# Narrow attention heads, software-pipelined: the next tile's first scores amid the products with V, the 1/sum and the projection one tile later, keys and queries in other PSUM banks

## The chip, the cores and the metric

The kernel runs on one core of a Trainium2 chip, as one program. The metric is the device time of one execution in microseconds (us). The engines are TensorE (PE; its weight loads are shown as PEld), VectorE (DVE), ScalarE (ACT), GpSimd (POOL) and SyncE (SP). SP computes nothing; it issues most of the DMAs. PSUM is the memory that matmuls write to, in banks; all the other on-chip data stands in SBUF.

## The reference, cut to what matters

Four layers run on x of shape (4, 512, 128) with a context of shape (4, 154, 128). Each layer is a cross attention and then a mixture of eight experts, both added to x. The change touches the attention of layer 1 alone:

```python
def _L1_xattn_ref(values, keys, queries, mask, Wv, Wk, Wq, Wo, bo):
    HEADS = 16                                   # E = 128, so D = 8
    v = values.reshape(N, -1, H, D)              # values = keys = context
    k = keys.reshape(N, -1, H, D)
    q = queries.reshape(N, Sq, H, D)             # queries = layernorm(x)
    v = jnp.einsum('nlhd,od->nlho', v, Wv)
    k = jnp.einsum('nlhd,od->nlho', k, Wk)
    q = jnp.einsum('nqhd,od->nqho', q, Wq)
    energy = jnp.einsum('nqhd,nkhd->nhqk', q, k)
    energy = jnp.where(mask == 0, jnp.float32(-1e+20), energy)
    attn = jax.nn.softmax(energy * (1.0 / E ** 0.5), axis=3)
    out = jnp.einsum('nhqk,nkhd->nqhd', attn, v).reshape(N, Sq, E)
    return out @ Wo.T + bo
```

The feed-forward part behind it sends every token to the best of eight experts (layer 1) or the best two (layers 0, 2, 3), with gate logits, a rank within the expert, and a weighted sum of what comes back.

## The kernel before, in words

**Tiles.** An attention works on tiles of 128 queries: four tiles (NI = 4) in each of four batches (B = 4), sixteen in all. Layer 1 has the narrow heads (8 dims each), layers 2 and 3 the wide ones (64 dims); they have a period function each, and share the class `Tile`. What a narrow tile goes through:

- `score(g)`, three groups: 6, 6 and 4 heads into one buffer `sc` of two PSUM banks. PE first writes the additive mask by a product with the identity (L1137) and then adds the queries times the keys (L1146). The keys `kz` stand eightfold, each copy masked to one head's dims of the eight in its half.
- `most(g)`: DVE takes the negated maximum over the 154 keys (L291, result `nm`).
- `exp(g)`: one ScalarE exponential for each head (L305), with the row's sum in `rs`.
- `short()`: ScalarE copies the last 26 keys of all heads together (L316). `inverse()`: DVE takes 1/sum (L327).
- `replicate()`: PE transposes 1/sum (L332), DVE copies it out of PSUM (`rT`, L334), SP sends it to DRAM eightfold (`rd`, L339) and back into SBUF (`rep`, L340), so that each of the 128 output rows has its head's 1/sum.
- `turn_ends()`, `turn(n)`, n = 0 to 3: PE transposes the probabilities, four 128x128 blocks into one bank `tr` (L355, L368). `take_ends`, `take(n)`: DVE copies the bank to SBUF (`tails`, `pT`; L261).
- `by_v_ends()`, `by_v(n)`: PE multiplies by the values into one bank `av` (L387, L405).
- `scaled()`: DVE multiplies by 1/sum (`aT`, L412). `project()`: PE multiplies by Wo (L422). `residual()`: DVE adds the bias and then x (L1160, L1161).

**PSUM.** Three pools share the banks: `ps_sc`, two buffers of two banks, `ps_tr` and `ps_av`, two buffers of one bank each. Who asks for a buffer waits until the one given out two calls earlier has been read.

**Order.** `attend_all` writes the order of PE, ACT and DVE by hand (`tc.manual_schedule`): each of these engines takes its instructions in program order, while SP's and POOL's are placed by a scheduler with a simulated time. `narrow_period(new, old, nxt, ...)` is one step of the loop over tiles: it does the rest of tile `new` (its groups 1 and 2; its group 0 was scored in the period before), the transposes and products of the tile before it, `old`, and the first scores of the tile after it, `nxt`. Four callbacks put other work into a period:

- `middle()` and `after()` each take one step of the work beside the attention (`beside.step`): the combine of the layer before for batches 2 and 3 (L953), the statistics of the layernorm (L224), the routing of the first half (gate logits L665, rank matmuls L692 and L694, choice and weights on DVE).
- `parts()` prepares the next batch, one part for each tile of the batch now running: `masks` (load L1091, conversion to an additive mask `madd` L1093), `xn` and `values` (L1111 to L1126), `xnT` (the transposed normalized x), and `keys_queries` (L1101 to L1109). This last one multiplies the context by Wk and x by Wq into the two banks of one `sc` buffer; DVE spreads the keys out under the head masks (`kz`, L1107) and ScalarE scales the queries (`qT`, L1109).
- `queries()` does nothing in this layer.

After the loop, outside the part with the order by hand, a last `narrow_period(None, last)` does the transposes, products and projection of the sixteenth tile, and the scheduler mixes it with the first steps of the experts.

Of the kernel before, what the change touches and what calls it, by code (L numbers as in the profile page):

```python
# [13 lines left out]
AF = mybir.ActivationFunctionType  # L14
ALU = mybir.AluOpType
# [6 lines left out]
S2 = 154  # L22
# [24 lines left out]
def tile_xattn_moe_stack(ctx: ExitStack, tc: tile.TileContext, a: dict, out: bass.AP):  # L47
# [10 lines left out]
    nc = tc.nc  # L58
# [37 lines left out]
    def bc(ap, axis, n):  # L96

        v = ap.unsqueeze(axis)
        shape = list(v.shape)
        shape[axis] = n  # L100
        return v.to_broadcast(shape)
# [42 lines left out]
    mask8 = const.tile([P, 8], F32, name="mask8")  # L144
# [42 lines left out]
    ctxT = const.tile([P, B, S2], F32, name="ctxT")  # L187
# [241 lines left out]
    def nothing():  # L429
        pass  # L430

    def narrow_period(new, old, nxt=None, middle=nothing, queries=nothing, parts=nothing, after=nothing):

        if new:  # L440
            new.score(1)
        if old:
            old.turn_ends()
            old.turn(0)
        if new:
            new.most(1)
            new.exp(0)
            new.exp(1)
        if old:
            old.take_ends("v")  # L450
            old.take(0, "v")
            old.by_v_ends()
            old.turn(1)
            old.take(1, "v")
        if new:
            new.score(2)
        if old:
            old.turn(2)
            old.by_v(0)
            old.by_v(1)  # L460
        if new:
            new.most(2)
            new.exp(2)
        if old:
            old.take(2, "v")
            old.turn(3)
            old.by_v(2)
            old.take(3, "v")
            old.by_v(3)
            old.scaled(0)  # L470
        middle()
        parts()
        if nxt:
            nxt.score(0)
            nxt.most(0)
        if new:
            new.short()
            new.inverse()
        queries()
        if new:  # L480
            new.replicate()
        if old:
            old.project()
            old.residual()
        after()

    def wide_period(new, old, nxt=None, middle=nothing, queries=nothing, parts=nothing, after=nothing):

        if new:
            new.score(0)  # L490
            new.score(1)
        if old:
            old.by_v_ends()
        if new:
            new.most(0)
            new.most(1)
            new.exp(0)
        if old:
            for n in (1, 2):
                old.turn(n)  # L500
                old.take(n, "v")
            old.by_v(0)
            old.by_v(1)
            old.turn(3)
            old.take(3, "v")
            old.by_v(2)
        if new:
            new.score(2)
            new.exp(1)
            new.most(2)  # L510
            new.exp(2)
# [12 lines left out]
        if old:  # L524
            old.project()
            old.residual()
        if new:
            new.turn_ends()
            new.take_ends("s")
            new.turn(0)  # L530
            new.take(0, "s")
        after()
# [526 lines left out]
    def layer1_setup():  # L1059
        dh = D // H  # L1060
        scale = 1.0 / D**0.5
        bd = {}
# [22 lines left out]
        def prepare(b, found):  # L1085
# [13 lines left out]
                at.xnT = transposed(at.xn)  # L1099

            def keys_queries():  # L1101
                sc = ps_sc()
                nc.tensor.matmul(sc[:, 0, 0:S2], bd["Wk"], ctxT[:, b, :], start=True, stop=True)
                nc.tensor.matmul(sc[:, 1, :], bd["Wq"], at.xnT, start=True, stop=True)

                at.kz = p2.tile([P, 8, S2], F32, tag="k", name="kz")
                nc.vector.tensor_tensor(at.kz, bc(sc[:, 0, 0:S2], 1, 8), bc(mask8, 2, S2), ALU.mult)  # L1107
                at.qT = p3.tile([P, S], F32, tag="t8", name="qT1")
                nc.scalar.activation(at.qT, sc[:, 1, :], AF.Copy, scale=scale)  # L1109

            def values():  # L1111
                vp = ps_av()
# [162 lines left out]
    def attend_all(layer, prepare, found, at, beside):  # L1275

        old = None
        period = narrow_period if layer == 1 else wide_period
        with tc.manual_schedule(engines=ordered):
            new = Tile(at, 0)
            if layer == 1:
                new.score(0)
                new.most(0)
            for b in range(B):
                new_at = prepare(b + 1, found) if b < B - 1 else None
                for i in range(NI):  # L1290
                    at_n, i_n = (at, i + 1) if i < NI - 1 else (new_at, 0)
                    nxt = Tile(at_n, i_n) if at_n else None
                    step = nothing if (b, i) in ((0, 0), (0, 1), (2, 0)) else beside.step

                    def queries(i=i, at=at):
                        if i < NI - 1:
                            at.queries(i + 1)

                    def parts(i=i, new_at=new_at):
                        if new_at:  # L1300
                            for part in new_at.parts[i]:
                                part()
                            if i == NI - 1:
                                new_at.queries(0)

                    def after(b=b, i=i, step=step):
                        step()
                        if b == 1 and i == 0:
                            beside.finish()
                            found.update({k: stats(x[k], layer == 2) for k in range(2, B)})  # L1310

                    period(new, old, nxt, step, queries, parts, after)
                    if b == 2 and i == 0:
                        beside = Steps(route(layer, 0, *gates[layer]))
                    old, new = new, nxt
                at = new_at
        return beside.finish(), old

    out_v = out.rearrange("b (i p) d -> b p i d", p=P)
    prepare = setups[0]()  # L1320
# [3 lines left out]
    for layer in range(4):  # L1324
        w2 = load_down(layer)
        if layer == 0:
            routed, last = [attend_first(layer, prepare, found)], None
        else:
            routed, last = attend_all(layer, prepare, found, at, beside)
            routed = [routed]  # L1330
        row_transfers()
        if layer < 3:
            prepare = setups[layer + 1]()
        first = Steps(experts(layer, 0, routed[0], w2)).step(2)
        if last:
            (narrow_period if layer == 1 else wide_period)(None, last)
        second = Steps(route(layer, 1, *gates[layer]))
        while not second.done:
            second.step(2)
# [55 lines left out]
```

## Time and profile before

| What | Value |
|---|---|
| Median of 5 runs | 1323.34 us (1318.14 to 1331.25) |
| Profiled execution | 1324.8 us, its span 1322.9 us |
| Mean granted PE clock | 0.93 |
| PE busy | 1096.5 us (83%) |
| PEld busy | 902.0 us (68%) |
| DVE busy | 748.4 us (57%) |
| ACT busy | 589.2 us (45%) |
| POOL busy | 252.8 us (19%) |
| HBM traffic over the span | 95 GB/s |

Busy shares are means over a span in which layers with different limits follow each other; the stretch of the layer that the change touches has to be cut out by time. The granted clock is a share of PE's full speed: at 0.50 a matmul takes twice as long. In a list by lines, `aT<-av,rep` says that `aT` was computed from `av` and `rep`. In a list of waits and in a timeline, an arrow with an engine and a name says whose result ended the idle time. Lines such as L261 (copies) and L291 (maxima) belong to helpers which all attention layers use, so their totals hold layers 2 and 3 too.

### The profile page before, as it was taken

To read this page: it belongs to the slowest core of one execution; us is meant where nothing else is said; L and a number is where in the kernel's file an instruction comes from. 1 tells how busy PE (TensorE), PEld (TensorE's weight loads), DVE (VectorE), ACT (ScalarE), POOL (GpSimd) and SP (SyncE) were. 2 spreads that over 40 slices of the span, in tenths; PEclk is the share of its full clock that TensorE was granted. 3 is DMA by queue.
4 is the path that set the end of the run, shared out by engine and by line. 5 is a ranking of instruction groups with operands and counts; after the bars stand their busy time and mean duration, and the time that the engine had idled before them with its cause. 6 is when DMAs were issued, how large, how long until landed. Compare 5 with 4: busy or idle time off the path is not lost.

```text
span 1322.9 us, 26947 instructions
## 1 busy us (share of the span) xinstructions
PE 1096.5 (83%) x9435; PEld 902.0 (68%) x9435; DVE 748.4 (57%) x2057; ACT 589.2 (45%) x2290; POOL 252.8 (19%) x281
## 2 busy tenths in 40 slices
PE   4875987887777778898999999867899999899881
PEld 2765877764334446787787787756778888789781
DVE  5663645557667566343676767424367576746442
ACT  1213443455454445446566556222466565533230
POOL 2032213104000020221000004045040000402424
PEclk8887999998898789999999999889899999999996
DMA  7023675551001122543121223445331111235762
GB/s 221 1 69 108 188 229 156 164 182 45 18 10 37 41 64 67 154 121 95 40 48 35 51 53 105 112 136 155 121 74 33 48 36 34 83 89 157 204 184 63
DMA packets 136995, 126.80 MB, mean 96 GB/s; under 512 B 13466, under 2 KB 116511, under 8 KB 136479
## 3 DMA queue, kind: packets, MB, share of 16 engines
q1 hardware_dynamic: 129695, 110.39, 30.1%
q0 software_dynamic: 7168, 14.69, 3.8%
q8 instruction: 77, 1.26, 0.4%
q14 instruction: 55, 0.45, 0.1%
HBM read 101.31 MB, written 23.72 MB: 95 GB/s over the span
## 4 chain that ended last, share of the span: by engine, by line
PE 37%; DVE 7%; DMA 7%; issue 3%; ACT 3%; POOL 2%; SPq 0%; POOLq 0%; DVEq 0%; ACTq 0%
PE sc L608 5%; PE tr L368 4%; PE tr L422 4%; PE av L405 4%; PE sc L875 4%; DMA w<-in_up 4%; PE av L902 3%; PE sc L593 3%; PE av L387 2%; ACT probs L305 2%; DVE nm L291 2%; POOL yg L935 2%; PE sc L557 1%; DMA yg<-ybuf,su 1%; DVE aT L412 1%
## 5 line engine op out<-in xcount | busy, mean ns | idle before, releaser
L305 ACT ACTIVATE probs<-sc,nm 128x154 f32<-128x154 f32 x768 | 287.0, 403 | 167.9 <-DVE nm L291 167.7
L875 PE MATMUL sc<-tokT,w 128*128 128x128 f32 x1528 | 213.0, 288 | 32.2 <-DMA w<-in_up 25.6
L875 PEld LDWEIGHTS sc<-tokT,w 128*128 128x128 f32 x1528 | 191.9, 200 | 46.6 <-DMA w<-in_up 13.7
L291 DVE TENSOR_REDUCE nm<-sc 128x6 f32<-128x924 f32 x144 | 143.2, 1010 | 85.2 <-PE sc L608 49.7
L902 PE MATMUL av<-w,hT 128*128 x1160 | 172.5, 283 | 11.1 <-DVE hT L891 9.2
L305 ACT ACTIVATION_READ_ACCUMULATOR probs<-sc,nm 128x1 f32 x768 | 168.2, 219 | 0.0
L902 PEld LDWEIGHTS av<-w,hT 128*128 128x128 f32 x1160 | 149.2, 194 | 21.5 <-DVE hT L891 13.3
L935 POOL DMA_INDIRECT yg<-ybuf,su x112 | 106.8, 954 | 277.0 <-DMA rd<-rT 63.7
L233 POOL TENSOR_TENSOR rstd<-ve,nhalf 128x4 f32<-128x4 f32 x32 | 33.2, 1038 | 617.6 <-DVE ve L231 496.7
L721 POOL DMA_INDIRECT buf<-xn,su x112 | 108.5, 969 | 169.5 <-DVE hT L891 40.6
L261 DVE COPY pT<-tr 128x512 f32<-128x512 f32 x160 | 107.3, 687 | 50.0 <-PE tr L368 45.6
L368 PE MATMUL tr<-ident,probs 128*128 128x128 f32 x768 | 121.3, 289 | 0.7 <-DVE rT L334 0.7
L405 PE MATMUL av<-pT,vm 128*64 128x128 f32 (+1 forms) x1536 | 102.7, 284 | 8.8 <-DVE pT L261 8.7
L890 ACT ACTIVATE eg<-sc,w 128x128 f32<-128x128 f32 x184 | 66.3, 367 | 96.3 <-DVE hT L891 72.1
L368 PEld LDWEIGHTS tr<-ident,probs 128*128 128x128 f32 x768 | 85.2, 145 | 29.2 <-issue 13.0
L891 DVE SCALAR_TENSOR_TENSOR hT<-sc,w,eg 128x128 f32<-128x128 f32 x184 | 63.0, 348 | 54.1 <-ACT eg L890 51.7
L910 DVE COPY ys<-av 128x128 f32<-128x128 f32 x168 | 48.5, 289 | 77.9 <-PE av L902 67.4
L405 PEld LDWEIGHTS av<-pT,vm 128*64 128x64 f32 (+1 forms) x1536 | 65.3, 127 | 35.7 <-issue 18.4
L608 PE MATMUL sc<-kT,qT 64*128 64x154 f32 x1024 | 86.0, 306 | 3.5 <-ACT probs L305 3.5
L608 PEld LDWEIGHTS sc<-kT,qT 64*128 64x128 f32 x1024 | 70.4, 187 | 14.4 <-issue 9.9
L593 PE MATMUL sc<-xnT,wq 128*128 128x128 f32 x512 | 71.1, 297 | 2.5 <-ACT probs L305 2.5
L593 PEld LDWEIGHTS sc<-xnT,wq 128*128 128x128 f32 x512 | 65.2, 206 | 7.9 <-issue 3.9
(252 smaller groups left out, 1466.8 us busy)
## 6 DMA issues: line engine op xcount, KB each, us to landing
w<-in_up SPq DMA_DIRECT2D x46, 516.0 KB
w<-in_up SPq DMA_DIRECT2D x76, 258.0 KB
rep<-rd SPq DMA_DIRECT2D x64, 256.0 KB
ybuf<-ys SPq DMA_DIRECT2D x168, 64.0 KB
tok<-buf SPq DMA_DIRECT2D x36, 256.0 KB
w<-in_down SPq DMA_DIRECT2D x3, 2048.0 KB
w<-in_up SPq DMA_DIRECT2D x46, 128.0 KB
buf<-zero SPq DMA_DIRECT2D x2, 1472.0 KB
```

The costliest lines, as they stand in the source:

```text
L261: return nc.vector.tensor_copy(o, i)
L291: nc.vector.tensor_reduce(self.at.heads(self.nm, g, n), self.sc[g][:, :, 0 : n * S2].rearrange("p j (s k) -> p j s k", s=n), AX.X, ALU.max ...
L305: nc.scalar.activation(self.pr[:, h, :], self.sc[g][:, j, s * S2 : (s + 1) * S2], AF.Exp, bias=self.nm[:, h : h + 1], accum_out=self.rs[:, ...
L368: nc.tensor.transpose(q[:, t * P : (t + 1) * P], self.pr[:, h, 0:P], ident)
L405: nc.tensor.matmul(av[rows, cols], v, self.pT[n][:, t, :], start=False, stop=last)
L593: nc.tensor.matmul(sc[:, c // 4, c % 4 * P : (c % 4 + 1) * P], wq[:, c * P : (c + 1) * P], at.xnT[:, i * P : (i + 1) * P], start=True, sto ...
L608: nc.tensor.matmul(sc[:, j, s * S2 : (s + 1) * S2], at.qT[i][rows, c, :], at.kT[rows, c, :], start=True, stop=True)
L721: ins = nc.gpsimd.indirect_dma_start(out=buf[half], out_offset=bass.IndirectOffsetOnAxis(ap=su[:, t : t + 1], axis=0), in_=xns[t // NI][:, ...
L875: nc.tensor.matmul(dst, w[:, at : at + P], xT, start=True, stop=True)
L890: nc.scalar.activation(g, sc[:, 1, fc * P : (fc + 1) * P], AF.Silu, bias=b1)
L902: nc.tensor.matmul(y[:, 0:D], hT[:, fc, :], w2[:, bass.ds(e, 1), fc, :].rearrange("p o d -> p (o d)"), start=(fc == 0), stop=(fc == nf - 1),)
L935: ins = nc.gpsimd.indirect_dma_start(out=yg[:, t, :], out_offset=None, in_=ybuf[half], in_offset=bass.IndirectOffsetOnAxis(ap=su[:, t : t ...
```

## The change

`narrow_period` has its statements in another order and takes a further tile, `older`, the one before `old`.

- The next tile's first scores and their maximum come after the second product with V of `old`, ahead of its last group of transposes. They came after all the products.
- 1/sum is still taken by DVE at the end of a tile's own period; its transpose, its copy and the two DMAs (`replicate`) come early in the next period. `project` and `residual` come one period after `scaled`, ahead of `replicate`.
- `new.most(1)` and `new.exp(0)` come ahead of the transposes of `old`, and `new.exp(1)` after the copy of its second group. The transposes and products of `old` alternate in another order.
- `parts()` comes ahead of `new.exp(1)`; it came after `middle()`. `middle()` and `after()` now have only statements of ScalarE and DVE for the new tile (`short`, `inverse`) between them.
- `keys_queries` takes its products from a `ps_tr` and a `ps_av` buffer in place of the two banks of a `ps_sc` buffer.
- `attend_all` hands over two tiles; after the last period the sixteenth tile is projected in a step of its own.

```diff
-    def narrow_period(new, old, nxt=None, middle=nothing, queries=nothing, parts=nothing, after=nothing):
+    def narrow_period(new, old, nxt=None, middle=nothing, queries=nothing, parts=nothing, after=nothing, older=None):
         if new:
             new.score(1)
-        if old:
-            old.turn_ends()
-            old.turn(0)
-        if new:
             new.most(1)
             new.exp(0)
-            new.exp(1)
+        if older:
+            older.project()
+            older.residual()
         if old:
+            old.replicate()
+            old.turn_ends()
             old.take_ends("v")
+            old.turn(0)
             old.take(0, "v")
             old.by_v_ends()
             old.turn(1)
             old.take(1, "v")
+        parts()
         if new:
+            new.exp(1)
             new.score(2)
-        if old:
-            old.turn(2)
-            old.by_v(0)
-            old.by_v(1)
-        if new:
             new.most(2)
             new.exp(2)
         if old:
+            old.by_v(0)
+            old.turn(2)
             old.take(2, "v")
+            old.by_v(1)
+        if nxt:
+            nxt.score(0)
+            nxt.most(0)
+        if old:
             old.turn(3)
+            old.take(3, "v")
             old.by_v(2)
-            old.take(3, "v")
             old.by_v(3)
             old.scaled(0)
         middle()
-        parts()
-        if nxt:
-            nxt.score(0)
-            nxt.most(0)
         if new:
             new.short()
             new.inverse()
         queries()
-        if new:
-            new.replicate()
-        if old:
-            old.project()
-            old.residual()
         after()
...
             def keys_queries():
-                sc = ps_sc()
-                nc.tensor.matmul(sc[:, 0, 0:S2], bd["Wk"], ctxT[:, b, :], start=True, stop=True)
-                nc.tensor.matmul(sc[:, 1, :], bd["Wq"], at.xnT, start=True, stop=True)
+                k, q = ps_tr(), ps_av()
+                nc.tensor.matmul(k[:, 0:S2], bd["Wk"], ctxT[:, b, :], start=True, stop=True)
+                nc.tensor.matmul(q, bd["Wq"], at.xnT, start=True, stop=True)
...
-                nc.vector.tensor_tensor(at.kz, bc(sc[:, 0, 0:S2], 1, 8), bc(mask8, 2, S2), ALU.mult)
+                nc.vector.tensor_tensor(at.kz, bc(k[:, 0:S2], 1, 8), bc(mask8, 2, S2), ALU.mult)
...
-                nc.scalar.activation(at.qT, sc[:, 1, :], AF.Copy, scale=scale)
+                nc.scalar.activation(at.qT, q, AF.Copy, scale=scale)
...
-                    period(new, old, nxt, step, queries, parts, after)
+                    period(new, old, nxt, step, queries, parts, after, older)
...
-                    old, new = new, nxt
+                    older, old, new = old, new, nxt
...
-        return beside.finish(), old
+        return beside.finish(), old, older
...
-        if last:
-            (narrow_period if layer == 1 else wide_period)(None, last)
+        if layer == 1:
+            narrow_period(None, last, older=late)
+            last.project()
+            last.residual()
+        elif last:
+            wide_period(None, last)
```

More of the change, by code (lines that the diff above doesn't have):

```diff
@@ L479, in narrow_period, with wide_period @@
         queries()
-        if new:
-            new.replicate()
-        if old:
-            old.project()
-            old.residual()
         after()
-    def wide_period(new, old, nxt=None, middle=nothing, queries=nothing, parts=nothing, after=nothing):
+    def wide_period(new, old, nxt=None, middle=nothing, queries=nothing, parts=nothing, after=nothing, older=None):
         if new:
@@ L1275, in attend_all @@
     def attend_all(layer, prepare, found, at, beside):
-        old = None
+        old = older = None
         period = narrow_period if layer == 1 else wide_period
@@ L1328, in tile_xattn_moe_stack @@
         else:
-            routed, last = attend_all(layer, prepare, found, at, beside)
-            routed = [routed]
+            result, last, late = attend_all(layer, prepare, found, at, beside)
+            routed = [result]
         row_transfers()
```

## The prediction, made before the changed kernel had run

> **What bounds the kernel.** The page says where the edit lives: lines L381, L1146, L1160 belong to the narrow attention, and the view by line places them between 289 and 527 us, 238 of the 1322.9 us of the span. The windows view of its middle shows that no engine is full there (columns: window, length, then busy us with counts for PE, PEld, DVE, ACT, POOL, then granted PE clock, DMA share, GB/s):
>
> ```profile
> 300.00:500.00 200.00, 153.29 (x1208) 83.14 (x1206) 135.72 (x309) 96.69 (x462) 28.14 (x29) 0.89 0.14 36
> ```
>
> PE 77%, DVE 68%, ACT 48%: the stage is a chain. The waits of 300 to 512 us (who waited for whom: total, times, longest) name its links:
>
> ```profile
> ACT probs L305 <- DVE nm L291: 85.7, 43, 5.9
> DVE nm L291 <- PE sc L1146: 30.6, 37, 2.4
> DVE pT L261 <- PE tr L368: 15.0, 34, 1.4
> PE av L381 <- DVE tails L261: 13.1, 12, 3.5
> ```
>
> ScalarE waits longest, but it is not last: it is free early in every period. What decides is the hand-over between PE and DVE, to be seen in the timeline of DVE over one ordinary period (start, duration, in brackets the idle time before and its releaser):
>
> ```profile
> 403.56 0.29 DVE L412 TENSOR_TENSOR aT<-av,rep 128x128 f32<-128x128 f32 x1 [0.55 <-PE av L405]
> 403.77 0.47 DVE L1093 TENSOR_SCALAR madd<-mi 128x616 bf16<-128x616 int32 x1
> 405.02 1.12 DVE L291 TENSOR_REDUCE nm<-sc 128x6 f32<-128x924 f32 x1 [0.77 <-PE sc L1146]
> 406.05 0.24 DVE L327 RECIPROCAL rinv<-rs 128x16 f32<-128x16 f32 x1
> 406.75 0.28 DVE L334 COPY rT<-tr 16x128 f32<-16x128 f32 x1 [0.45 <-PE tr L332]
> ...
> 407.30 0.29 DVE L1161 TENSOR_TENSOR x<-x,res 128x128 f32<-128x128 f32 x1
> 408.35 1.12 DVE L291 TENSOR_REDUCE nm<-sc 128x6 f32<-128x924 f32 x1 [0.76 <-PE sc L1146]
> 409.38 0.68 DVE L261 COPY tails<-tr 104x512 f32<-104x512 f32 x1
> 409.98 0.68 DVE L261 COPY pT<-tr 128x512 f32<-128x512 f32 x1
> 411.17 0.69 DVE L261 COPY pT<-tr 128x512 f32<-128x512 f32 x1 [0.51 <-PE tr L368]
> 412.16 0.80 DVE L291 TENSOR_REDUCE nm<-sc 128x4 f32<-128x616 f32 x1 [0.30 <-PE sc L1146]
> 412.88 0.68 DVE L261 COPY pT<-tr 128x512 f32<-128x512 f32 x1
> 413.90 0.69 DVE L261 COPY pT<-tr 128x512 f32<-128x512 f32 x1 [0.34 <-PE tr L368]
> 415.14 0.29 DVE L412 TENSOR_TENSOR aT<-av,rep 128x128 f32<-128x128 f32 x1 [0.55 <-PE av L405]
> ```
>
> A period is 415.14 - 403.56 = 11.58 us, and DVE waits for PE seven times in it, 3.7 us in all. The sixteen periods are not alike: from one product with 1/sum (aT) to the next the DVE timeline gives 12.1, 12.5, 16.6, 14.8, 12.1, 12.1, 14.6, 11.6, 16.8, 18.3, 17.2, 15.7, 17.6, 11.6.
>
> **Ordinary period.** I lay each engine's instructions in their order; each starts when its engine is free and its input and buffer are there. From the same rows: six heads' scores 1.59 to the maximum's start (403.43 to 405.02), PE free after 1.45; four heads' scores 1.07; four transposes 0.48, readable after 0.7; a maximum frees DVE after 1.03 or 0.72, a copy after 0.60; six exponentials 6 x 0.367 = 2.2. The old order so laid gives 11.37, 0.2 under the trace.
>
> The new order, from the start of a tile's second scores: first maximum read at 1.58, exponentials of group 1 from 2.73. PE has the older tile's projection and the 1/sum transpose done at 1.8, but the transposes of the tails need the PSUM buffer that the residual frees, and the residual stands behind that maximum: residual 2.61, tails' transposes 2.96, tails copied 3.66, copies 4.26 and 5.47, third scores 5.24, third maximum 6.43, third copy 7.31, the next tile's first scores 7.37 to 8.82, their maximum 8.95 (DVE idles 1.04 for it), last copy only then at 9.98, last products 10.72, next period 11.08. So the exponentials of the next tile start early, at 10.1, but DVE's wait for first scores (0.77) only moves in front of the last copy. Gain 0.29; over 14 intervals **-4.1**. First tile: its 1/sum now stands before its transposes, +1.1; last tile: nobody's scores amid its products, -1.9. **-0.8**.
>
> **Keys and queries.** Old: 14.62 - 11.58 = 3.0 more, since the next first scores waited for kz (1.44), then qT (0.60). New: two buffers, qT no longer behind kz, first scores a third of a period later; what stays is 1.35 of DVE and 1.03 of PE, 2.2 by the same laying. The old order so laid has 3.6, so the gain is 0.8 to 1.4; I take 1.2, three times: **-3.6**.
>
> **Transposed x.** In two of three batches ScalarE copies it (0.59), now between two groups of exponentials; it waits there for PE until 5.4, the second group ends at 8.3 and frees the score buffer 0.9 late: +1.1 each, **+2.2**.
>
> **Mask.** The scheduled order puts madd after the second copy, in mid-period; it was last. Its load is issued by SP, behind the pair rd, rep of the tile before, which moves with the 1/sum into this period. SP's rows:
>
> ```profile
> 342.61 0.32 SPq L340 DMA_DIRECT2D rep<-rd  x1
> 345.47 0.39 SPq L1091 DMA_DIRECT2D mi<-in_mask_Bx1xSxS_if  x1
> ```
>
> Traffic follows until 348.1, 2.7 after the issue, and madd stood at 350.20: hidden. Now rT is at 3.2, rd 3.5, rep 2.4 to 3.6 later as in the rows of before, the mask issued at 6.2 to 7.4, there at 8.9 to 10.1, and DVE is at madd at 6.1. It stands, and the third maximum and every copy behind it; the idle times behind absorb about 1.2. 1.7 to 2.9, middle 2.3, for batches 2 and 3: **+4.6**.
>
> **Work beside.** Combines, statistics and routing have two places. Old: after aT (1.0 hidden under the first scores) and at the end (0.76 hidden under the second). New: both fall between aT and the first maximum, where 1.0 is free. Eight combines of 0.32 cost 2.6 - 1.0 = 1.6 (old row: 12.50 against 12.06); gate logits wait in front of the second scores for xnT's copy, the rank matmuls for DVE's selection. All such steps laid at full clock: old 19.4, new 24.4: **+5.0**.
>
> **1/sum and projection.** The same instructions, DMAs included: rd and rep of each tile go out one period later. From rT to aT it was 8.4 (406.75 to 415.14), now 8.05; the pair needs 0.3 + 2.4 to 3.6 + 1.6 = 4.3 to 5.5. Hidden; without that cover each excess us costs 14. After the last tile, rd goes behind a weight load and rep behind a store, but PE still holds three blocks of the experts: aT about 12.4 after tile 14's, as before: **0**, from -1 to +3.
>
> **Clock.** The trace has the clock at 0.50 in 13 stretches of 3.4 us, each after a stretch with PE nearly idle:
>
> ```profile
> 396.50:399.91 3.41, 2.60 (x26) 1.75 (x26) 2.63 (x4) 2.41 (x14) 0.00 (x0) 1.00 0.16 24
> 399.91:403.32 3.41, 2.98 (x44) 1.67 (x44) 2.46 (x4) 2.22 (x11) 0.00 (x0) 1.00 0.41 112
> 417.00:420.41 3.41, 0.07 (x2) 0.00 (x0) 3.38 (x15) 0.00 (x0) 1.85 (x2) 0.99 0.32 131
> 420.41:423.82 3.41, 2.73 (x9) 1.22 (x9) 2.67 (x11) 2.33 (x12) 0.00 (x0) 0.50 0.14 19
> ```
>
> Steps beside cost 29.1 in the trace (the intervals above less the plain ones), 19.4 at full clock: 0.75 a stretch. The new order loses stretches at keys and queries and gets some where combines and routing keep PE waiting up to 4.9. Taken equal: **0**, from 6 to 20 of them: -5 to +5.
>
> The Trainium skill ("TensorE: Matmul & The Clock Gate", Part 4: PE-mode transpose) speaks against the change: transposes do not count as PE being busy, and between 1.7 and 5.2 of the new period there is little else. The row 396.50 has 1.90 of 2.60 us in transposes and keeps 1.00 afterwards, so I go by the row; by the rule one stretch a period, some +10. The clock rival below is that case, priced from rows.
>
> **Sum.** -4.1 - 0.8 - 3.6 + 2.2 + 4.6 + 5.0 = +3.3 on the profiled execution's 1324.8. That is 1.5 above the median, so 1323.3 + 3.3 = **1326.6**. One per cent, 13.2 us, is about what a measurement of this kernel can tell from no change.
>
> **Rivals.**
> Clock (slower): the period's clump of transposes lets the clock drop in every ordinary period. For: a full group of scores at half clock took 0.98 + 1.91 (421.69, 422.60) against 0.55 + 1.05, 1.3 more. Against: the row 396.50. From one stretch per period it decides: 14 x 0.75 to 1.3, middle +14: 1341.
> No chain (faster): ScalarE's 85.7 us of waits do matter, and DVE's idle 4.1 is half filled: 14 x -1.7 more: 1303. For: the largest wait. Against: the old order laid without it meets the trace within 2%.
> Cover holds: the mask lands early and the steps beside hide as before, 4.6 + 5.0 less: 1317.
> 1/sum late (the edit exposes what it moves): the pair takes over 8 us; 1 us over is +14, 1341. Against: no wait on rep in 16.
>
> **Numbers.** Forecast 0.60, clock 0.14, cover 0.14, no chain 0.08, late 1/sum 0.04. Slower by over 1%: most of clock, half of late, the forecast's edge, 0.15; faster: 0.07; the rest 0.78. From 1314 (cover with fewer slow stretches) to 1340 leaves out no chain, the upper half of clock and of late: 0.17.
>
> **What would show it.** DVE at aT every 11.0 to 11.4 in ordinary periods; before the first of a tile's maxima a wait on PE of about 1.0, now followed by the last copy; madd waiting for its DMA about 3 us twice; no ScalarE wait over 3 us in plain periods; aT never on rep. Wrong if ordinary periods come near 10 or if the clock is 0.50 in them.

## The result, and the profile after

The changed kernel takes 1326.13 us (median of 50 runs, 1316.55 to 1339.05) where the kernel before, now with 92 runs, takes 1320.94 (1309.94 to 1334.36). The ratio is 1.0048, 95% interval 1.0035 to 1.006: 6.3 us slower, 4.6 to 7.9, and less than one per cent. Forecast were 1326.6 and +3.3. That 1326.6 and 1326.13 lie so close is in part luck: the forecast started from a median of five runs, 1323.34, which is 2.4 above that of 92, and its +3.3 is below the 4.6 to 7.9 measured.

The profiled execution took 1332.92 us, 6.8 above its kernel's median, so its total isn't used; what is compared is the stage that the change touches. In both profiles I take it from the first product with 1/sum (`aT`, of the first tile) to that of the fifteenth: 203.5 us before, 206.1 after.

The windows view of the changed kernel for the same 200 us as before (columns: window, length, busy us with counts for PE, PEld, DVE, ACT, POOL, then granted PE clock, DMA share, GB/s):

```profile
300.00:500.00 200.00, 157.41 (x1181) 82.22 (x1184) 131.97 (x305) 92.95 (x450) 28.18 (x29) 0.87 0.13 36
```

PE is busier by 4.1 us with fewer instructions, and its mean clock went from 0.89 to 0.87; DVE and ACT are less busy. The stage is still a chain. The waits of 300 to 512 us (who waited for whom: total, times, longest):

```profile
ACT probs L305 <- DVE nm L291: 62.0, 24, 6.1
...
DVE nm L291 <- PE sc L1142: 32.6, 29, 2.4
ACT qT L1105 <- PE av L1100: 22.0, 3, 9.1
...
PE tr L355 <- DVE res L1156: 20.5, 14, 3.1
...
ACT xnT L92 <- PE tr L248: 17.2, 3, 9.2
```

ScalarE's largest wait fell from 85.7 to 62.0 us, but ScalarE waits no less in all: its waits for the queries (`qT`) and the transposed x (`xnT`), which it now copies between two groups of exponentials, rose from 10.4 and 3.0 us before to 22.0 and 17.2. The line on `res` is new: 14 times PE stands with the tails' transposes until the residual has given back its PSUM buffer, the link that the prediction put at 2.61 of its period. The timeline of DVE shows one period whole (start, duration, in brackets the idle time before and its releaser; the stretch has a granted clock of 1.00 throughout):

```profile
364.52 0.29 DVE L412 TENSOR_TENSOR aT<-av,rep 128x128 f32<-128x128 f32 x1 [0.55 <-PE av L405]
364.73 0.24 DVE L327 RECIPROCAL rinv<-rs 128x16 f32<-128x16 f32 x1
365.98 1.12 DVE L291 TENSOR_REDUCE nm<-sc 128x6 f32<-128x924 f32 x1 [1.00 <-PE sc L1142]
367.01 0.28 DVE L1156 TENSOR_TENSOR res<-tr,bo 128x128 f32<-128x128 f32 x1
367.33 0.29 DVE L1157 TENSOR_TENSOR x<-x,res 128x128 f32<-128x128 f32 x1
367.54 0.27 DVE L334 COPY rT<-tr 16x128 f32<-16x128 f32 x1
368.09 0.69 DVE L261 COPY tails<-tr 104x512 f32<-104x512 f32 x1 [0.28 <-PE tr L355]
368.70 0.68 DVE L261 COPY pT<-tr 128x512 f32<-128x512 f32 x1
369.89 0.69 DVE L261 COPY pT<-tr 128x512 f32<-128x512 f32 x1 [0.51 <-PE tr L368]
370.50 0.68 DVE L88 COPY xnT<-tr 128x512 f32<-128x512 f32 x1
371.31 0.80 DVE L291 TENSOR_REDUCE nm<-sc 128x4 f32<-128x616 f32 x1
372.25 0.69 DVE L261 COPY pT<-tr 128x512 f32<-128x512 f32 x1
374.09 1.12 DVE L291 TENSOR_REDUCE nm<-sc 128x6 f32<-128x924 f32 x1 [1.15 <-PE sc L1142]
375.12 0.68 DVE L261 COPY pT<-tr 128x512 f32<-128x512 f32 x1
376.35 0.29 DVE L412 TENSOR_TENSOR aT<-av,rep 128x128 f32<-128x128 f32 x1 [0.55 <-PE av L405]
```

The forecast had DVE idle 1.04 ahead of the next tile's first maximum, with the last copy behind it; it idles 1.15, and the copy follows at 375.12. The first fifteen products with 1/sum, read from such timelines, are apart by (before, in the prediction: 12.1, 12.5, 16.6, 14.8 and so on) 12.5, 15.6, 15.7, 13.2, 11.8, 13.2, 14.0, 13.1, 17.2, 20.1, 15.5, 14.6, 20.2, 9.5 us.

The mask stood as foretold. First SP's queue, then DVE's timeline:

```profile
395.92 0.33 SPq L340 DMA_DIRECT2D rep<-rd  x1
396.29 0.43 SPq L1087 DMA_DIRECT2D mi<-in_mask_Bx1xSxS_if  x1
```

```profile
399.38 0.48 DVE L1089 TENSOR_SCALAR madd<-mi 128x616 bf16<-128x616 int32 x1 [3.77 <-DMA mi<-in_mask_Bx1xSxS_if]
```

The load is issued 6.74 us after the period's aT (389.55), behind `rep`, and DVE stands 3.77 us; the other time it was 2.41. What comes next is in the windows around it:

```profile
396.00:399.40 3.40, 3.22 (x30) 1.41 (x22) 0.02 (x1) 0.00 (x0) 0.00 (x0) 1.00 0.40 112
399.40:402.60 3.20, 0.43 (x8) 0.16 (x8) 3.20 (x5) 1.97 (x9) 0.00 (x0) 1.00 0.00 0
402.60:406.00 3.40, 3.16 (x14) 0.84 (x14) 0.64 (x3) 2.40 (x13) 0.00 (x0) 0.50 0.00 0
```

With DVE late, PE has 0.43 us of work in 3.2, and the next 3.4 us run at half clock: the wait is paid a second time. In the tile behind it DVE waits 2.22 us for the next first scores, where it waits 1.00 in the tile shown above.

### The profile page after: what moved, and what is told of

Its sections match the earlier page's. It is cut to its first block, busy times and chain, and to the rows that moved or that the text cites. A ratio compares the mean times of both kernels' runs of the same rounds, so it can differ in the third digit from the quotient of the medians.

```text
span 1330.9 us, 26960 instructions
## 1 busy us (share of the span) xinstructions
PE 1112.9 (84%) x9435; PEld 910.4 (68%) x9435; DVE 747.9 (56%) x2057; ACT 587.2 (44%) x2290; POOL 252.6 (19%) x281
## 4 chain that ended last, share of the span: by engine, by line
PE 57%; DVE 14%; DMA 11%; issue 7%; ACT 6%; POOL 3%; SPq 2%; POOLq 0%; DVEq 0%; ACTq 0%
PE sc L871 9%; DMA w<-in_up 6%; PE tr L368 6%; PE av L405 5%; PE sc L604 5%; PE av L898 5%; PE tr L422 4%; DVE nm L291 3%; ACT probs L305 3%; PE sc L589 3%; PE sc L1142 3%; DMA yg<-ybuf,su 2%; PE av L387 2%; POOL yg L931 2%; PE tr L355 2%
## 5 line engine op out<-in xcount | busy, mean ns | idle before, releaser
L368 PE MATMUL tr<-ident,probs 128*128 128x128 f32 x768 | 124.9, 295 | 1.7 <-DVE rT L334 1.6
L405 PE MATMUL av<-pT,vm 128*64 128x128 f32 (+1 forms) x1536 | 106.3, 286 | 17.3 <-DVE pT L261 16.9
```

Source lines behind the costliest of these rows:

```text
L368: nc.tensor.transpose(q[:, t * P : (t + 1) * P], self.pr[:, h, 0:P], ident)
L405: nc.tensor.matmul(av[rows, cols], v, self.pT[n][:, t, :], start=False, stop=last)
```

## The experiments

All of them touch the narrow attention only. They ran on three chips, numbered 1 to 3 in the table, each chip with runs of the kernel before beside them. On chips 2 and 3 the kernel before takes some 90 to 100 us more (medians of 1320.46, 1421.55 and 1410.47 us on the three), so a total is compared within its chip only, and stages across chips with care; the last section says more on it. "Stage" is first aT to fifteenth. "Laid" is the same stage by the method of the prediction (each engine's instructions in their order with the durations of the trace of before, at full clock), done for the whole order at once; it is an estimate, of which only the sum is given here. For mask_early and all_three, whose edit to the mask had no effect, it is that of the order without it. "Stretches" is the time at half clock within the stage over 3.41 us. "Remote" is idle time in the stage whose releaser the trace gives as remote, with no event of this core that ends it; where two engines have it, both bounds are given (VectorE's alone, and the sum).

| Kernel (chip) | Total, ratio to before | Laid | Stage | Stretches | Remote |
|---|---|---|---|---|---|
| before | 1 | 192.4 | 203.5 | 12 | 0 |
| changed | 1.0048 (1.0035 to 1.006) | 192.3 | 206.1 | 15 | 0 |
| kq_only (1) | 0.9984 (0.9952 to 1.0017) | 189.6 | 198.0 | 9 | 0 |
| late_only (1) | 0.9929 (0.9903 to 0.9954) | 185.1 | 196.6 | 12 | 0 |
| scores_only (1) | 1.0073 (1.0042 to 1.0105) | 187 to 190 | 212.0 | 19 | 0 |
| exp_again (1) | 1.0074 (1.0042 to 1.0105) | | 210.6 | 16 | 0 |
| mask_early (2) | 0.9946 (0.9921 to 0.9972) | 192.3 | 212.6 | 15 | 9.7 |
| turn3_first (2) | 0.9803 (0.9772 to 0.9834) | 177.8 | 198.7 | 19 | 6 to 10 |
| turn3_mid (2) | 0.98 (0.9764 to 0.9837) | 170.1 | 190.4 | 13 | 8 to 13 |
| all_three (2) | 0.9802 (0.9769 to 0.9835) | 170.1 | 189.1 | 16 | 3 to 7 |
| after_here (3) | 0.997 (0.9938 to 1.0003) | 192.3 | 210.3 | 14 | 4.7 |
| mask_later (3) | 0.995 (0.9921 to 0.9979) | 188.8 | 209.4 | 15 | 8 to 12 |
| three_parts (3) | 0.9901 (0.9865 to 0.9937) | 184.1 | 208.9 | 18 | 8 to 13 |
| best (3) | 0.9786 (0.9748 to 0.9824) | 166 | 185.7 | 14 | 6 to 10 |

What stands above the laid time goes with the stretches: (203.5 - 192.4) / 12 = 0.93 us for each in the kernel before, 0.92 in the changed one, 0.93 in kq_only, 0.96 in late_only; 1.1 to 1.3 in scores_only. These are one profile each, the count changes from one execution to the next, and no run changed the clock alone: that the stretches carry the whole difference is an estimate.

### Each part of the change alone, on the kernel before

**Keys and queries in other banks.**

```diff
-                sc = ps_sc()
-                nc.tensor.matmul(sc[:, 0, 0:S2], bd["Wk"], ctxT[:, b, :], start=True, stop=True)
-                nc.tensor.matmul(sc[:, 1, :], bd["Wq"], at.xnT, start=True, stop=True)
+                k, q = ps_tr(), ps_av()
+                nc.tensor.matmul(k[:, 0:S2], bd["Wk"], ctxT[:, b, :], start=True, stop=True)
+                nc.tensor.matmul(q, bd["Wq"], at.xnT, start=True, stop=True)
```

> The kernel before, with keys and queries taken from a ps_tr and a ps_av buffer and nothing else changed. Measured against the kernel before; the stage is taken from the first product with 1/sum (aT of tile 1) to the fifteenth, 203.5 us in the profile of before. My theory (a chain that PE and DVE hand to and fro): the three periods with keys and queries lose what the scaled queries waited for the spread keys, 0.6 to 1.5 us each, -2.8 in all; the scores still wait for the spread keys. Rival (the banks carried the whole gain that the prediction gave to keys and queries): -3.6 or more. Rival (keys and queries were hidden by the first scores' own wait): 0.

The interval with keys and queries that has no other work in it went from 14.62 to 13.23 us. So 1.4 of the 3.0 that they cost above an ordinary period of 11.58 goes with the banks alone, and that fits the theory's 0.6 to 1.5. The total lies between -6.3 and +2.2 us, too wide to tell -2.8 from 0; the stage has three stretches fewer, which at 0.93 each is 2.8 of its 5.5.

**1/sum and projection one tile later.**

```diff
         if new:
             new.score(1)
+        if older:
+            older.project()
+            older.residual()
         if old:
+            old.replicate()
             old.turn_ends()
...
         queries()
-        if new:
-            new.replicate()
-        if old:
-            old.project()
-            old.residual()
         after()
```

> The kernel before, with the transpose, the copy and the DMAs of 1/sum and the projection one tile later, ahead of the transposes of the tile, and nothing else changed. My theory: PE no longer waits for 1/sum between first and second scores of a tile, so that the second scores follow at once; laid in order, an ordinary period goes from 11.4 to 10.6 us, the whole stage loses 7.3 us of 203.5. Rival (1/sum late: the trip through DRAM is exposed): aT waits for rep, and the stage becomes longer, 1 us per tile or +14. Rival (the prediction's term, that 1/sum and projection cost and gain nothing by themselves): 0.

The theory holds: 0.9929, 8.9 us by the medians (6.1 to 12.8 by the interval), and 6.9 in the stage. The waits of PE show why. In the kernel before, from 300 to 512 us:

```profile
PE tr L332 <- DVE rinv L327: 23.2, 14, 4.0
```

In late_only, from 300 to 512 us:

```profile
PE tr L355 <- DVE res L1159: 9.0, 13, 2.1
...
PE tr L332 <- DVE rinv L327: 2.1, 1, 2.1
```

Before, PE stood 14 times and 23.2 us in all with the transpose of 1/sum until DVE had taken 1/sum. In late_only that is nearly gone; a shorter wait of the tails' transposes for the residual has come in, 9.0 us, the one that takes 20.5 in the changed kernel, where the residual stands behind the second maximum. The timeline of PE at the start of an ordinary period of late_only:

```profile
397.54 0.56 PE L1136 MATMUL sc<-madd,ident_b 128*128 128x462 bf16 x2
398.03 1.04 PE L1145 MATMUL sc<-kz,qT 64*128 64x462 f32 x4
399.01 0.56 PE L1136 MATMUL sc<-madd,ident_b 128*128 128x462 bf16 x2
399.50 1.05 PE L1145 MATMUL sc<-kz,qT 64*128 64x462 f32 x4
400.48 0.49 PE L422 MATMUL tr<-woT,aT 128*128 128x128 f32 x2
400.81 0.27 PE L332 MATMUL tr<-ident,rinv 128*16 128x128 f32 x1
```

The second scores start 1.47 us after the first, and the transpose of 1/sum stands behind both. Before, it stood between them (in the period that the prediction shows, the two maxima start 3.33 apart, at 405.02 and 408.35; here it is 2.62). The ordinary period went from 11.58 to 10.84. No product with 1/sum waited for `rep`.

**The next tile's first scores amid the products.**

```diff
             old.take(2, "v")
+        last_part()
+        if nxt:
+            nxt.score(0)
+            nxt.most(0)
+        if old:
             old.turn(3)
...
-        if nxt:
-            nxt.score(0)
-            nxt.most(0)
```

`last_part()` prepares keys and queries in a batch's last tile; the other parts of the preparation stay where they were.

> The kernel before, with the next tile's first scores and their maximum between the third copy and the last transposes of a tile, keys and queries of the next batch just ahead of them, and nothing else changed. My theory: the periods with keys and queries lose 3 us each, ordinary ones nothing or up to 0.8 more (the last copy stands behind the maximum), -2 to -5 in the stage. Rival (ScalarE's waits for a maximum decide): its exponentials start 1.7 us earlier in each period, -24.

A miss: 1.0073, 8.5 us more in the stage. The order itself costs an ordinary tile nothing: a period at full clock takes 11.22 us, against 11.58 before. But 19 stretches ran at half clock where before there were 12. The very next tile shows it, with nothing beside it but the mask's conversion. Windows of that kernel:

```profile
402.40:405.81 3.41, 1.87 (x25) 0.92 (x25) 2.37 (x7) 2.33 (x12) 0.00 (x0) 1.00 0.01 2
...
412.64:416.05 3.41, 1.88 (x24) 0.74 (x20) 2.30 (x4) 2.54 (x12) 0.00 (x0) 1.00 0.00 0
416.05:419.46 3.41, 3.01 (x9) 1.22 (x9) 1.12 (x5) 0.70 (x4) 0.00 (x0) 0.53 0.14 19
```

At the period's start PE has its last products behind it and waits for 1/sum (1.05 us) with nothing else to do. The windows are cut near the clock's own steps, not at them: the clock falls at 416.26, and the 3.41 us just before that hold 1.67 us of PE work, those from 402.61 hold 1.87 and are followed by full clock. Such a period lies on an edge, which isn't sharp: in the kernel before, 3.41 us with 1.94 us of PE work are followed by full clock once (from 403.26) and by half clock once (from 485.18). This period took 13.14 us. Why the stretches became more, beyond this one, is not shown. Starting ScalarE earlier bought nothing, against the rival.

**ScalarE made slower in the changed kernel.**

```diff
-            for s in range(min(3, 8 - 3 * g)):
-                for j in range(2):
+            twice = [(0, 0)] if self.nb == 1 else []
+            for s, j in twice + [(s, j) for s in range(min(3, 8 - 3 * g)) for j in range(2)]:
+                if True:
```

> The changed kernel, with the first exponential of each of a tile's three groups done twice, the same values into the same place: 0.4 to 0.6 us more ScalarE work ahead of each group's end, 1.1 to 1.8 us per tile, nothing else changed. My theory: ScalarE waits 1 to 2.7 us for each maximum and its results are asked for later than they are ready, so the stage (206.1 us from the first aT to the fifteenth in the profile of the changed kernel) grows by 0 to 3 us. Rival (no chain; ScalarE's waits decide): 14 times 1.1 or more, +15 to +25.

Each group became 0.51 us longer, 1.5 per tile, 21 over the fourteen intervals. The stage grew by 4.5, one stretch among it, more than the 0 to 3 expected and far less than the rival's 15 to 25; the total by 3.4 against the changed kernel's own ratio (1.0074 to 1.0048), with intervals that overlap. The period shown above took 11.83 again, to the hundredth. Longer by about 0.5 became those in which ScalarE has a copy of its own to do: transposed x (12.52 to 13.03), scaled queries (13.20 to 13.71), routing (17.23 to 17.77). ScalarE's exponentials don't decide the period; where it has a copy to do, that stands in line behind them.

### Steps of the changed kernel undone or moved

**The mask's load earlier.**

```diff
+            mi = p2.tile([P, NI, S2], I32, tag="vt", name="mi")
+            nc.sync.dma_start(mi, mask_in[b])
+
             def masks():
-                mi = p2.tile([P, NI, S2], I32, tag="vt", name="mi")
-                nc.sync.dma_start(mi, mask_in[b])
```

> The changed kernel, with the load of the next batch's mask (mi) issued when the batch is prepared, one tile's period earlier in program order, instead of just ahead of its conversion; nothing else changed. Stage from the first aT to the fifteenth, 206.1 us in the profile of the changed kernel. My theory: madd no longer waits for its DMA (2.4 and 3.8 us there), and the two tiles after it lose 1.7 each, -3.5 at full clock (the prediction's term says -4.6). Rival (cover holds: what stands behind madd waits for something else anyway): 0 to -1.

This didn't do what it was made for, and says nothing on the theory: the load still stood behind `rep` (issued at 403.52 and 403.88 in its trace), and madd waited 6.1 us in two waits, against 6.2. The kernel's text has a possible second reason: `mi` shares its buffers with the values' tails (`vt`), so the load may not start until PE's tails' products of the tile before have read them. In this trace those products ended at 401.91, ahead of both issues, so the run doesn't separate SP's order from the buffer; the prediction named only the first. Its ratio to the kernel before is 0.9946 on this chip, where the changed kernel itself wasn't run; as its edit had no effect, it stands in for that kernel there.

**The mask converted one tile later,** which takes the wait away without a buffer more:

```diff
...
-            at.parts = ((masks,), (xn, values), (xnT,), (keys_queries,))
+            at.parts = ((load,), (masks, xn, values), (xnT,), (keys_queries,))
```

> The changed kernel, with the next batch's mask loaded where it is now (first tile of a batch) and converted one tile later, ahead of that tile's layernorm; nothing else changed. It takes away what madd waits for, since mask_early did not: there the load still stood behind the last reader of its buffer, the tails' products of the tile before. My theory: the two waits of 2.4 and 3.8 us go, the stage loses 3.5 at full clock (the prediction's term says 4.6). Rival (cover holds): 0 to -1.

 

> The changed kernel itself, unaltered, so that the three others of this call can be compared with it on their own chip, and for a second look at the stretches at half clock. My theory: the stage (first aT to fifteenth) is 192.3 us at full clock as laid, as in the kernel before (192.4), and what it differs from that by is 0.9 us for each stretch at half clock, 12 to 16 of them: 203 to 207. Rival (the stretches belong to the one execution that was profiled): fewer than 10 of them and under 202.

Against the changed kernel on the same chip the two intervals with the mask went from 14.71 to 12.82 and from 13.96 to 11.40, 1.9 and 2.6 less; of the first, part is a stretch at half clock that after_here has there (346.3 to 349.7) and mask_later hasn't. The interval behind the second one went from 13.09 to 11.83, since the stretch at half clock (407.7 to 411.1 in after_here) is gone. The whole stage fell by 0.9 only, with more remote waits in it, and the total by 3.0 (medians 1406.49 and 1403.48), with intervals that overlap. So the two tiles speak for the theory and against "cover holds", and stage and total can't tell them apart. With the mask gone there is also a tile with nothing beside it:

```profile
397.41 0.29 DVE L412 TENSOR_TENSOR aT<-av,rep 128x128 f32<-128x128 f32 x1 [0.55 <-PE av L405]
...
404.70 0.69 DVE L261 COPY pT<-tr 128x512 f32<-128x512 f32 x1
406.54 1.12 DVE L291 TENSOR_REDUCE nm<-sc 128x6 f32<-128x924 f32 x1 [1.15 <-PE sc L1144]
407.57 0.68 DVE L261 COPY pT<-tr 128x512 f32<-128x512 f32 x1
408.81 0.29 DVE L412 TENSOR_TENSOR aT<-av,rep 128x128 f32<-128x128 f32 x1 [0.55 <-PE av L405]
```

The ordinary period of the new order is 408.81 - 397.41 = 11.40 us, against 11.58 before.

after_here had 14 stretches, as expected, but 210.3 us in the stage and not 203 to 207; 0.92 for each stretch and the 4.7 us of remote waits, which nobody expected, would take that back to 192.7. On this chip the changed kernel is 0.997 of the kernel before, 0.9938 to 1.0003: the half per cent by which it is slower elsewhere isn't there.

**The last transposes and their copy ahead of the next tile's first scores.**

```diff
             old.by_v(1)
+        if old:
+            old.turn(3)
+            old.take(3, "v")
         if nxt:
             nxt.score(0)
             nxt.most(0)
         if old:
-            old.turn(3)
-            old.take(3, "v")
             old.by_v(2)
```

> The changed kernel, with the last group of transposes and its copy ahead of the next tile's first scores instead of behind them; nothing else changed. My theory: DVE does the last copy while PE does the first scores, where it stood idle 1.0 to 1.2 us, and the last products no longer wait for a copy behind the maximum: an ordinary period goes from 11.1 to 10.0 or 10.4 us, the stage from 206.1 to about 190 (-14.5 at full clock, and fewer stretches at half clock rather than more). Rival (ScalarE decides): the next tile's exponentials start 0.5 us later in their period, so 0 or longer. Rival (the clock decides: periods with PE kept waiting lose what was won): -5.

0.9803 of the kernel before, and 18 us less by the medians than mask_early, which stands in for the changed kernel on this chip (1394.34 and 1412.56). The period of the timeline above takes 10.64 in place of 11.83. The stage is 198.7 us, more than the 190 expected, and the stretches became more, 19, not fewer; with the remote waits they are more than the difference. DVE's wait, which the change had only moved in front of the last copy, is now filled by it.

**One of the two steps beside put back under cover.**

```diff
             old.take(3, "v")
+        middle()
         if nxt:
...
             old.scaled(0)
-        middle()
```

> As turn3_first, and the first of the two steps of work beside (middle) put behind the last copy, ahead of the next tile's first scores, instead of behind the product with 1/sum; nothing else changed. My theory: combines, statistics and routing again have two places with cover, as in the kernel before: 8 us less than turn3_first at full clock, about 180. Rival (the steps hide as well at the one place): the same as turn3_first. Rival (the rows that the combine adds have not landed by then): DVE waits for the gathered rows once, and 2 to 5 us of it are lost again.

The stage fell by 8.3, which is the number expected, but not at full clock: it has six stretches fewer, about 5.6 us at 0.93 each, and some 2 us more of remote waits. In the total nothing is seen: 0.98 against 0.9803, each to within 0.4%, and the medians differ by 3.3 us. No wait of DVE for the gathered rows came in. So the sign is supported by the stage, and the price of the one place isn't settled.

**All three:** turn3_mid with the edit of mask_early.

> turn3_mid with the mask loaded early as in mask_early. My theory: the three are additive, 166 us at full clock for the stage, and 0.9 us for each stretch at half clock, of which there are 8 to 12: 173 to 178, 28 to 33 less than the changed kernel, 22 to 28 less than the kernel before. Rival (ScalarE decides): no faster than the kernel before.

Since its mask load stayed late as in mask_early, all_three is turn3_mid once more: 0.9802, and the same 6.1 us of waits for the mask.

### The three parts without the rest, and the best order

**Three parts.** late_only, kq_only and scores_only together, on the kernel before:

> The kernel before with the three named parts of the change and none of the rest: 1/sum and projection one tile later, the next tile's first scores and their maximum behind the third copy, keys and queries in the other banks (just ahead of those scores). Transposes, exponentials, preparation of the next batch and the two steps beside stay where they were. My theory: 184.1 us at full clock for the stage, 8.3 less than the kernel before and 8.2 less than the changed kernel, so that the gain of the parts was given back by the rest of the new order; and since PE no longer stands waiting for 1/sum, the stretches at half clock stay at 9 to 13 rather than the 19 of scores_only. Rival (first scores amid the products are what costs, as scores_only suggests): no faster than the kernel before.

0.9901 against 0.997 of the changed kernel on the same chip: 11 us by the medians (1395.10 and 1406.49), where 8.2 were expected. So the parts together are worth about 1%, and the rest of the new order (residual and transposes behind the second maxima, preparation in mid-period, both steps beside in one place) gave most of it back; which of these gave back how much isn't shown. Against the 0.9929 of late_only, on another chip, the two other parts add nothing that could be told from noise, and an ordinary period takes 11.28 here, 10.84 there. The forecast of the stretches was wrong, 18 and not 9 to 13: five of them lie from 489 to 507 us, around a remote wait of PE of 4.3 us, but three are also at the start, and whether this order has more of them by itself stays open.

**Best:** turn3_mid with the mask converted one tile later.

> turn3_mid with the mask converted one tile later as in mask_later. My theory: 170.1 at full clock for the stage of turn3_mid, some 166 here, plus 0.9 for each stretch at half clock, of which there are 8 to 13: 173 to 178, 28 to 33 less than the changed kernel and 25 to 30 less than the kernel before in the total. Rival (ScalarE decides): no faster than the kernel before.

0.9786 (0.9748 to 0.9824), against 0.997 of the changed kernel on the same chip: it beats both, by the medians the kernel before by 33 us and the changed one by 29. Its stage, 185.7, is above the 173 to 178 expected; 14 stretches, one more than expected, and 6 to 10 us of remote waits, by the estimate above, account for that. A tile with nothing beside it on DVE:

```profile
399.44 0.28 DVE L412 TENSOR_TENSOR aT<-av,rep 128x128 f32<-128x128 f32 x1
...
406.29 0.69 DVE L261 COPY pT<-tr 128x512 f32<-128x512 f32 x1
407.23 0.69 DVE L261 COPY pT<-tr 128x512 f32<-128x512 f32 x1 [0.25 <-PE tr L368]
408.61 1.12 DVE L291 TENSOR_REDUCE nm<-sc 128x6 f32<-128x924 f32 x1 [0.68 <-PE sc L1145]
409.64 0.28 DVE L412 TENSOR_TENSOR aT<-av,rep 128x128 f32<-128x128 f32 x1
```

10.20 us: the maximum is followed by aT at once, because its products ran behind the scores on PE.

## Why the prediction was right

The total lay in the range and the sign was right, and so was what bounds the stage. The sum of the terms came out partly by luck, by two errors that cancel: the terms gave +3.3 where the two orders, laid whole, are equal, and the clock was put at 0 where it is +2.8 by the estimate. The size was low, 3.3 against 4.6 to 7.9.

- **The chain between PE and DVE.** Right. 1.5 us more of ScalarE per tile, 21 in all, added 4.5 to the stage and left the period shown alone (exp_again), while filling DVE's wait for PE took 18 us off the total (turn3_first). The rival "no chain" falls. That ScalarE's largest wait lost 24 us says little by itself, since its other waits grew as much.
- **Ordinary period.** Right in shape, wait by wait; 0.18 and not 0.29 are won in each (11.58 to 11.40), so -2.5 and not -4.1.
- **Keys and queries.** 14.62 to 13.20, of which 0.18 is the ordinary gain: 1.24, priced at 1.2. kq_only gets 1.4 with the banks alone.
- **Transposed x.** The tile with ScalarE's copy and nothing else new took 12.52, 1.1 above 11.40, as priced. The copy on DVE, taken as free, cost 0.4 (11.83).
- **Mask.** 4.5 us at its two tiles, part of it a stretch at half clock, priced at 4.6 at full clock. Behind it comes another such stretch, 1.3 at the second mask, which no term had.
- **Work beside.** +5.0 can't be read from one row. Undoing the move of one step took 8.3 off the stage (7.7 laid), with six stretches fewer, and nothing clear off the total: the sign is supported, the price open.
- **1/sum and projection.** The step that failed, as far as one did: "the same instructions", hidden, nothing lost. Nothing was lost, and no aT waited for `rep`; but alone this move wins 7 to 9 us. The prediction asked only what covers the moved work, not who had been waiting for it at the old place (PE, between first and second scores, 23.2 us in all). In the changed order the gain is inside the ordinary period, and another wait of PE, for the residual, takes 20.5 us in its stead.
- **Clock.** Mis-sized. Taken as equal, with a count of 13 stretches; the views give 15 from 288.7 to 526.6, 12 of them between the first aT and the fifteenth, and not each behind a PE nearly idle (1.94 us of work in the 3.41 from 485.18). The changed order has 15, and 14 in after_here, 15 in mask_early and 16 in exp_again; the kernels with the first scores in their old place (before, kq_only, late_only) have 12, 9 and 12. By the estimate, three stretches at 0.92 are +2.8, all of the 2.6 by which the stages differ. Laid in one go at full clock, the two orders are equal (192.4 and 192.3), where the terms, laid one by one, gave +3.3.
- **The clump of transposes.** The rival "clock in every ordinary period" falls: from 348.0 to 402.4 us, four tiles, the changed kernel has no stretch at half clock. The prediction's row from 396.50 is the sharper case: without its transposes it has 0.70 us of PE work, and 1.00 behind it, where 1.67 us in all were followed by half clock in scores_only. The Trainium skill ("TensorE: Matmul & The Clock Gate", Part 4: PE-mode transpose) says that a transpose doesn't count as PE being busy in the same way; here the traces differ from it, and the measurement decides. The traces list these transposes as matmuls with the identity.
- **After the last tile.** From the sixteenth aT to the first copy of layer 2's keys it took 63.8 us before, 66.0 after, 62.4 in exp_again with the same end: the price of 0 isn't contradicted.

What stays open: the stage from its first maximum to the sixteenth aT grew by 2.4 us in the two profiles, the total by 4.6 to 7.9. The rest isn't placed. The two traces drift apart by a further 4 or 5 us in layers whose code is the same, and single executions of one kernel differ by up to 24 us.

## What to carry to other kernels

When a step is moved, ask first who had been waiting for it where it stood; here that wait was worth more than all that the new place had to hide. Work put in mid-chain "for later use" (a load's conversion, a copy on a shared engine, a routing step) is free only where the chain idles, and a wait that leaves PE with little work can be paid again at half clock (here after 0.43 us of work in 3.2, and at times still after 1.67 to 1.94 in 3.41). Lay out two orders whole, instruction by instruction, rather than term by term: sums of single terms miss what they take from each other, +3.3 against 0 here.

## What was not expected of the hardware

On chips 2 and 3 the kernel before takes 90 to 100 us more than on chip 1, and the changed kernel 80 more on chip 3 than in its own 50 runs. The traces there have remote waits, which no event of the core ends: 78.6 us in after_here over the whole span, summed over the engines, 81.2 in best, 95.0 in turn3_mid, and none in the traces of chip 1 or in those of before and after. The waits of after_here hold two lines of it:

```profile
ACT hT L879 <- remote: 30.1, 5, 6.7
...
DVE ys L906 <- remote: 18.0, 4, 9.5
```

They strike experts and attention alike, the longest of these two lines 6.7 and 9.5 us. In best, the copy at 333.20 has stood 3.50 us, though the transposes that it copies ended at 329.92. What these waits are, and whether they are all of the 90 us, the runs don't show. They do show that an effect of half a per cent differs from chip to chip: 1.0048 (1.0035 to 1.006) and 0.997 (0.9938 to 1.0003) are the same kernel.
